# The first step of a fused two-layer kernel: the order of its loads, products, sums and copies

## The chip, the cores and the metric

The kernel runs on one core of a Trainium2 chip. A core has five engines with instruction streams of their own: PE (TensorE, matmuls and transposes), DVE (VectorE), ACT (ScalarE), POOL (GpSimd) and SP (SyncE, which here only issues DMAs). Each works through its stream in order and waits for semaphores of the others. The metric is device time in microseconds of one execution, lower is better. Before the change it was 2017.71 us (median of three, 2015.79 to 2018.18).

## The reference

The input has 2048 rows (4 sequences of 512) of 512 float32 values. Two layers are computed; each normalizes the rows and adds an attention and a mixture of experts that both read the normalized rows:

```python
xn = _layernorm(x)
x = x + _L0_attn_ref(xn, ...) + _L0_ffn_ref(xn, ...)
xn = _layernorm(x)
x = x + _L1_attn_ref(xn, ...) + _L1_ffn_ref(xn, ...)
```

The change touches the first normalization and the first attention. That attention has 16 heads of 128 and projects the normalized rows with Wq, Wlk and Wlv to queries, local keys and local values, each 2048 wide, with RMS norms and a rotation of queries and keys:

```python
q = (hidden_states @ Wq + bq).reshape(Bq, Sq, NH, D).transpose(0, 2, 1, 3)
q = apply_rope(rmsnorm(q, qn_w), pos)
lk = apply_rope(rmsnorm((hidden_states @ Wlk + blk).reshape(...)..., kn_w), pos)
lv = (hidden_states @ Wlv + blv).reshape(Bq, Sq, NH, D).transpose(0, 2, 1, 3)
```

## The kernel before

**Staging.** The rows lie in 16 tiles of 128 (`acc`), four tiles to a sequence. A tile is normalized to `xn` by `layernorm` (L226): statistics on DVE (L232 to L235), a power on POOL (L236), and the scaling on DVE (L247) or, where `scaled` is set, on ACT (L245, with one more POOL operation, L238). Its rows are then stored to DRAM (L250), transposed on PE (L255) and copied by ACT into `xnT` (L256). Rows 0 to 3 go the DVE way, rows 4 to 15 the ACT way.

The first attention runs in 32 steps: 8 groups of two heads, and in each group the four sequences. Step i projects one sequence on one group's 768 columns, makes scores and contexts, and meanwhile projects for step i+1. Jobs for other parts, such as the normalization of rows 8 to 15 in steps 0 and 1, are hung between (`jobs0`, L962 on).

**The projection.** `project` (L656) halves the 512 rows and the 512 inner elements and multiplies the four blocks with seven products in place of eight, by sums of blocks of x (`sums_x`, L667: `xs[0]` to `xs[3]`) and of the weights (`combine_weights`, L112: t3, b1 in place, t2, t4). A product (L681) covers 128 rows at a time (`c` is 0 or 1) and accumulates two matmuls, each of which the profile shows as two instructions. Products one and two (`first`, L710) read the plain blocks; six and seven (`second`, L720) read `xs1` with t2 and `xs2` with t3; four (`third`, L726) reads t4; five and three follow. After products one and two, `finish` (L688) squares the six heads' rows on ACT (L581), raises to −0.5 on POOL (L583, L584), rotates on DVE (L591 to L594) and scales on ACT (L695). `turn_queries` (L697) transposes the queries on PE.

**Order.** The program is written engine by engine in Python order, but a planner reorders the instructions of an engine by its estimate of when their inputs are there. `tc.keep_in_program_order(ins)` forbids that for one instruction: it stays behind the instruction written just before it on its engine. Before the change, of the opening, the norms of rows 0 to 3, their transposes, the four weight sums, the tables (`tables`, L201, POOL) and some POOL operations are pinned; products, sums of x, squares, copies and all later statistics are free.

The opening is written as: start rows 0 and 1, scale the norm weights (L197), products p1(0), p2(0), p1(1), then `rest` (L1082: rows 2 and 3, tables, and the loads of everything that follows), the adds of the first projection, p2(1), `finish(0)`, then

```python
entry_tables()
combine_weights(0)
bound()
unrotated()
sums_x()
first_logits(0)
second(0)
turn_queries(0)
second(1)
third()
```

**Queues.** Nearly all loads are issued by SP in written order: row 0, first half of wA, row 1, the norm weights qn_w and kn_w, second half of wA, bias A, rows 2 and 3, cos, sin, the two halves of wB, bias B, small ones, wr (the weights of the router's logits, `first_logits`, L941), then the stores of `xn` and the other loads.

**PSUM.** Banks are shared by tag: three "mm" (products), three "sc" (logits, scores), two "tr" (transposes).

Of the kernel before, what the change touches and what calls it, by code (L numbers as in the profile page):

```python
# [29 lines left out]
E = 8  # L30
# [19 lines left out]
def two_layers(ctx: ExitStack, tc: tile.TileContext, a: dict, out: bass.AP, large: bass.AP):  # L50
# [37 lines left out]
    def load_block(g, nm, between=None):  # L88
# [3 lines left out]
        for f in range(2):  # L92
            nc.sync.dma_start(out=w[:, ts(f, 2), :],
                              in_=a[nm][g, ts(f, 2 * P), :].rearrange("(k p) c -> p k c", p=P))
            if between:
                between(nm, f)
# [15 lines left out]
    def combine_weights(g):  # L112
# [4 lines left out]
        t2_, t3_, t4_ = (wpool.tile([P, 2, 3 * D], F32, tag=f"wT{x}", name=f"wT{x}_{g}", bufs=1) for x in (2, 3, 4))  # L117
        for o, x, y in ((t3_, b2_, b1), (b1, b1, w_a[:, 0:2, :]), (t2_, b2_, b1), (t4_, t2_, a2)):
            tc.keep_in_program_order(V.tensor_tensor(o, x, y, ALU.subtract))  # L119
        d = G.tensor_tensor(b2[:, 1, :], b2[:, 1, :], b2[:, 0, :], ALU.subtract)  # L120
        if g == 0:
            tc.keep_in_program_order(d)
        sums_w[g] = t2_, t3_, t4_
# [28 lines left out]
    def load_between(nm, f):  # L152
        if nm == "wA" and f == 0:
            load_x(1)
            for w, src in enumerate(("qn_w", "kn_w")):
                nc.sync.dma_start(out=nw[:, w, :], in_=a[src].partition_broadcast(P))

    def load_tables():
        for n in range(2, TC):
            load_x(n)  # L160
# [3 lines left out]
    load_x(0)  # L164
    w_ = [load_block(0, "wA", load_between)]
# [3 lines left out]
    w_.append(load_block(0, "wB", load_between))  # L169
# [5 lines left out]
    wr = load_few(sp0, "wr", 1 + E, a["wr9"])  # L175
# [50 lines left out]
    def layernorm(n, pool, bank, scaled=False, bufs=None):  # L226
# [5 lines left out]
        pin(V.bn_stats(st, acc[:, n, :]))  # L232
# [8 lines left out]
        def rows():  # L241
            tag = "ctx" if n in (2, 3) else "xn"
            xn = made["xn"] = (wk0 if n in (2, 3) else pool).tile([P, HID], F32, tag=tag, name=f"xn_{n}", bufs=bufs)
            if scaled:
                A.activation(xn, acc[:, n, :], AF.Identity, scale=mv[:, 1:2], bias=mv[:, 0:1])  # L245
# [6 lines left out]
        def turn():  # L252
# [3 lines left out]
            A.copy(xnT[:, :, ts(n, P)], tr.rearrange("p (k t) -> p k t", k=KC))  # L256
# [3 lines left out]
    def logits(b, w, m, pool, name, get, bank):  # L260
# [6 lines left out]
        A.copy(lr, lp)  # L267

        def turn():
            tr = bank("tr", f"trg_{name}_{b}")  # L270
            for t in range(TC):
                PE.transpose(tr[:, ts(t, P)], lr[:, ts(t, P)], ident)
# [303 lines left out]
    def squares(x, n, pool, name, extra=1.0):  # L576

        sq = pool.tile([P, D], F32, tag="sq", name=f"sq_{name}", bufs=1)
        ss = small.tile([P, n], F32, tag=f"ss{n}", name=f"ss_{name}", bufs=4)
        for h in range(n):  # L580
            A.activation(sq, x[:, h, :], AF.Square, accum_out=ss[:, h : h + 1])  # L581
        pin = tc.keep_in_program_order if name == "0_0" else (lambda x: x)
# [73 lines left out]
    def project(i):  # L656
# [10 lines left out]
        def sums_x():  # L667
# [1643 lines left out]
```

## Time and profile before

| | |
|---|---|
| median of three runs | 2017.71 us (2015.79 to 2018.18) |
| profiled execution | 2017.76 us |
| its span, first to last instruction | 2016.0 us |
| mean granted TensorE clock | 0.997 |
| DVE, ACT, POOL busy | 1513.7, 866.7, 743.2 us |
| DMA moved | 267.26 MB, 133 GB/s |
| PE busy in 0 to 36 us, 36 to 82 us, 82 to 145 us | 22.00, 42.91, 62.97 us |

The profile is that of one execution. "Busy" sums the time in which an engine worked on instructions. In a timeline row the numbers are start and duration in us, then engine, line, operation, the tile written and read, shapes and how many were merged; in brackets stands the idle time before it and who ended it. A window row gives the busy time of each engine in a stretch with the count of instructions.

### The profile page before, as it was taken

What the parts mean: (1) busy time and instruction counts of PE and PEld (TensorE: products, weight loads), DVE (VectorE), ACT (ScalarE), POOL (GpSimd) and SP (SyncE); (2) the same over time, 40 slices, a digit from 0 to 9 for tenths busy, and PEclk for the clock granted to TensorE, in tenths of its full rate; (3) what the DMA queues carried; (4) which work ended last, traced back from release to release, by engine and by line L of the source; (5) the groups of instructions that cost most, each with busy time, mean ns of one, the idle gap of its engine ahead of it and who ended that gap; (6) DMA issues with size and microseconds to landing.
All of it is one profiled execution on the core that took longest, in us unless ns stands there. A gap on an engine that the chain in (4) does not pass through costs nothing.

```text
span 2016.0 us, 28488 instructions
## 1 busy us (share of the span) xinstructions
PE 1976.1 (98%) x9358; PEld 1241.5 (62%) x9358; DVE 1513.7 (75%) x3696; ACT 866.7 (43%) x2600; POOL 743.2 (37%) x761
## 2 busy tenths in 40 slices
PE   7999999999999999999999999999999999999998
PEld 4666666777767767776667766666434445445443
DVE  7889977777776777787767788788696755565886
ACT  4554444444444444444444445545234432333332
POOL 4422244443332333333442344445204432333551
PEclk8999999999999999999999999999999999999999
DMA  7102133432433333344452222321307775775441
GB/s 257 70 32 63 33 131 111 155 116 95 139 111 122 120 123 136 106 134 158 152 182 99 96 65 82 90 80 70 128 22 247 258 257 194 266 254 173 155 155 69
DMA packets 98908, 267.26 MB, mean 133 GB/s; under 512 B 14400, under 2 KB 27840, under 8 KB 87488
## 3 DMA queue, kind: packets, MB, share of 16 engines
q0 software_dynamic: 27072, 148.91, 21.9%
q1 hardware_dynamic: 70528, 114.34, 16.9%
q10 hardware_dynamic: 1152, 2.10, 0.3%
q8 instruction: 77, 1.26, 0.3%
q14 instruction: 79, 0.65, 0.1%
HBM read 222.05 MB, written 42.73 MB: 131 GB/s over the span
## 4 chain that ended last, share of the span: by engine, by line
PE 84%; DVE 8%; ACT 2%; POOL 1%; issue 1%; DMA 1%; DVEq 0%; ACTq 0%; POOLq 0%
PE p L681 24%; PE hp_r L534 13%; PE st L773 4%; PE op L848 4%; PE st L1344 3%; PE po L1482 3%; PE cx L1358 3%; PE qp L1320 3%; PE sp L764 2%; PE ox L879 2%; PE o L1427 2%; PE ca L817 2%; PE trm_r L522 1%; PE oz L879 1%; PE trq L701 1%; PE cc L820 1%
## 5 line engine op out<-in xcount | busy, mean ns | idle before, releaser
L534 PE MATMUL hp_r<-we_r,xT_r 128*128 128x512 f32 (+1 forms) x592 | 224.7, 596 | 2.7 <-ACT xT_r L524 2.2
L486 POOL DMA_INDIRECT xr_r<-xnd,rows_r x72 | 87.7, 1218 | 345.1 <-PE trm_r L522 307.4
L781 POOL TENSOR_TENSOR lT<-lT,lmask 128x512 f32<-128x512 f32 (+1 forms) x128 | 152.4, 1199 | 122.5 <-ACT lT L777 122.1
L681 PE MATMUL p<-wT,x 128*128 128x384 f32 x512 | 179.7, 494 | 0.8 <-DVE wT L119 0.8
L681 PE MATMUL p<-wB,x 128*128 128x384 f32 x512 | 175.9, 488 | 0.8 <-DVE u L737 0.8
L681 PE MATMUL p<-wA,xnT 128*128 128x384 f32 x512 | 173.8, 490 | 0.7 <-DVE u L716 0.4
L581 ACT ACTIVATE sq<-qb 128x128 f32<-128x128 f32 x384 | 118.9, 310 | 91.7 <-DVE qb L730 45.6
L1346 ACT ACTIVATE pT<-st 128x1024 f32<-128x1024 f32 x128 | 123.3, 1015 | 59.3 <-PE st L1344 51.1
L534 PEld LDWEIGHTS hp_r<-we_r,xT_r 128*128 128x128 f32 (+1 forms) x592 | 83.1, 170 | 98.8 <-issue 92.4
L681 PEld LDWEIGHTS p<-wT,x 128*128 128x128 f32 x512 | 94.6, 193 | 63.3 <-issue 6.5
L681 PEld LDWEIGHTS p<-wB,x 128*128 128x128 f32 x512 | 93.7, 190 | 64.4 <-issue 9.6
L681 PEld LDWEIGHTS p<-wA,xnT 128*128 128x128 f32 x512 | 94.9, 192 | 62.1 <-DVE u L716 3.5
L695 ACT ACTIVATE qb<-qb,ss 128x128 f32<-128x128 f32 x256 | 81.9, 390 | 107.7 <-POOL ss L584 104.6
L524 ACT COPY xT_r<-trm_r 128x512 f32<-128x512 f32 x72 | 41.8, 580 | 194.3 <-PE hp_r L534 183.2
L773 PE MATMUL st<-qkT 128*128 128x256 f32 (+1 forms) x512 | 114.6, 354 | 1.5 <-ACT qkT L708 1.5
L777 ACT ACTIVATE lT<-st,ss 128x256 f32<-128x256 f32 (+1 forms) x128 | 48.9, 444 | 151.7 <-PE st L773 151.7
L551 POOL DMA_INDIRECT row_r<-yd,slot_r x64 | 72.8, 1137 | 73.9 <-DMA yd<-yr_r 21.5
L773 PEld LDWEIGHTS st<-qkT 128*128 128x128 f32 x512 | 92.2, 190 | 12.0 <-ACT qkT L708 1.7
L584 POOL TENSOR_TENSOR ss<-ss,nhalf 128x6 f32<-128x6 f32 x64 | 96.1, 1502 | 5.3
L848 PE MATMUL op<-Wo,cT 128*128 128x512 f32 x208 | 93.9, 596 | 1.3 <-DVE lv L745 1.2
L583 POOL TENSOR_SCALAR ss<-ss 128x6 f32<-128x6 f32 x64 | 31.3, 489 | 166.3 <-ACT sq L581 165.9
L681 PE MATMUL p<-wT,xnT 128*128 128x384 f32 x256 | 88.1, 486 | 0.0
(385 smaller groups left out, 4627.9 us busy)
## 6 DMA issues: line engine op xcount, KB each, us to landing
x<-xsd SPq DMA_DIRECT2D x112, 256.0 KB, 3.1
yd<-yr_r SPq DMA_DIRECT2D x72, 256.0 KB, 4.9
wA<-in_wA SPq DMA_DIRECT2D x16, 384.0 KB, 3.5
wB<-in_wB SPq DMA_DIRECT2D x16, 384.0 KB, 7.3
xnd<-xn SPq DMA_DIRECT2D x24, 256.0 KB, 2.2
accd<-acc SPq DMA_DIRECT2D x18, 256.0 KB, 2.1
acc<-in_x SPq DMA_DIRECT2D x16, 256.0 KB, 5.8
Wo<-in_Wo SPq DMA_DIRECT2D x8, 512.0 KB, 3.6
```

The costliest lines, as they stand in the source:

```text
L486: G.indirect_dma_start(out=out, out_offset=None, in_=src, in_offset=at_rows(idx))
L534: PE.matmul(hp[ts(h, m), :], lhsT=xT[:, k, ts(h, m)], rhs=w[:, ts(k, HID)], start=(k == 0), stop=(k == KC - 1))
L551: G.indirect_dma_start(out=x, out_offset=None, in_=self.yd, in_offset=at_rows(self.r.slot[:, k, n : n + 1]))
L581: A.activation(sq, x[:, h, :], AF.Square, accum_out=ss[:, h : h + 1])
L584: pin(G.tensor_tensor(ss, ss, nhalf[:, 0:n], ALU.pow))
L681: PE.matmul(p, lhsT=x[:, k, ts(c, P)], rhs=w[:, k, :], start=(k == 0), stop=(k == 1))
L695: A.activation(x[:, j, :], x[:, j, :], AF.Copy, scale=sq[t][:, j : j + 1])
L773: PE.matmul(st[:, ds((t % 2) * 256, n)], lhsT=qkT[:, HG + h, ts(t, P)], rhs=qkT[:, h, ds(t * P, n)], start=True, stop=True)
L781: G.tensor_tensor(dst, dst, lmask.rearrange("p a w j -> p (a w j)")[:, 0:n], ALU.mult)
L848: PE.matmul(op, lhsT=cT[:, h, ts(t, P)], rhs=wo[:, h, :], start=(h == 0), stop=(h == HG - 1))
L879: PE.matmul(p[:, ts(c, 256)], lhsT=left[:, ts(c, P)], rhs=right, start=new and c == 0, stop=True, skip_group_check=True)
L1346: A.activation(pt[:, ts(pair, 2), :], st, AF.Exp, scale=SCALE1)
```

## The change

All edits concern the opening, except one.

- Loads: rows 0 to 3 are issued first; then wA, bias A, qn_w and kn_w, cos and sin, wB; wr ahead of bias B.
- Rows 1 and 3 are normalized with `scaled` set. The statistics of rows 0 and 1 are written ahead of both scalings, and the opening, with `scale_weights`, `tables` and `rest`, is written ahead of the products (`begin`).
- `first` takes a generator `parts`: the transposes of rows 2 and 3, sums of x and weight sums are written between the products and adds of step 0.
- `sevenths` makes both halves of p7, in "sc" banks, behind the first logits and ahead of `turn_queries` and p6; `second` then adds them from there.
- Pinned now in step 0: products, sums of x, the adds of the first projection, the first squares, ACT's copies of rows 0 to 3, the copy and transposes of the first logits.
- The exception: the first statistic (L232) of rows 8 to 15 is pinned.

The diff, with unchanged lines cut (the line numbers are in its hunk headers):

```diff
--- before.py
+++ after.py
@@ -85,15 +85,13 @@
...
         return t
-    def load_block(g, nm, between=None):
+    def load_block(g, nm):
         w = wpool.tile([P, KC, 3 * D], F32, tag=nm, name=f"{nm}_{g}", bufs=1 if nm == "wA" else 2)
...
                               in_=a[nm][g, ts(f, 2 * P), :].rearrange("(k p) c -> p k c", p=P))
-            if between:
-                between(nm, f)
         return w
...
@@ -109,18 +107,21 @@
...
         return wo
-    def combine_weights(g):
+    def combine_weights(g, which=(0, 1, 2, 3)):
         (w_a, w_b), b2 = groups[g]
         a2, b1, b2_ = w_a[:, 2:4, :], w_b[:, 0:2, :], w_b[:, 2:4, :]
-        t2_, t3_, t4_ = (wpool.tile([P, 2, 3 * D], F32, tag=f"wT{x}", name=f"wT{x}_{g}", bufs=1) for x in (2, 3, 4))
-        for o, x, y in ((t3_, b2_, b1), (b1, b1, w_a[:, 0:2, :]), (t2_, b2_, b1), (t4_, t2_, a2)):
-            tc.keep_in_program_order(V.tensor_tensor(o, x, y, ALU.subtract))
-        d = G.tensor_tensor(b2[:, 1, :], b2[:, 1, :], b2[:, 0, :], ALU.subtract)
-        if g == 0:
-            tc.keep_in_program_order(d)
-        sums_w[g] = t2_, t3_, t4_
+        if g not in sums_w:
+            sums_w[g] = [wpool.tile([P, 2, 3 * D], F32, tag=f"wT{x}", name=f"wT{x}_{g}", bufs=1) for x in (2, 3, 4)]
+        t2_, t3_, t4_ = sums_w[g]
+        for n, (o, x, y) in enumerate(((t3_, b2_, b1), (b1, b1, w_a[:, 0:2, :]), (t2_, b2_, b1), (t4_, t2_, a2))):
+            if n in which:
+                tc.keep_in_program_order(V.tensor_tensor(o, x, y, ALU.subtract))
+        if 3 in which:
+            d = G.tensor_tensor(b2[:, 1, :], b2[:, 1, :], b2[:, 0, :], ALU.subtract)
+            if g == 0:
+                tc.keep_in_program_order(d)
     sums_w, out_w, out_t = {}, {}, {}
...
@@ -149,30 +150,25 @@
...
     wcol = small.tile([P, 2], F32, tag="wcol", name="wcol", bufs=1)
-    def load_between(nm, f):
-        if nm == "wA" and f == 0:
-            load_x(1)
-            for w, src in enumerate(("qn_w", "kn_w")):
-                nc.sync.dma_start(out=nw[:, w, :], in_=a[src].partition_broadcast(P))
-
     def load_tables():
-        for n in range(2, TC):
-            load_x(n)
+        for w, src in enumerate(("qn_w", "kn_w")):
+            nc.sync.dma_start(out=nw[:, w, :], in_=a[src].partition_broadcast(P))
         nc.sync.dma_start(out=cos, in_=a["c_cos"][:, :, 0:R])
         nc.sync.dma_start(out=sin, in_=a["c_sin"])
-    load_x(0)
-    w_ = [load_block(0, "wA", load_between)]
+    for n in range(TC):
+        load_x(n)
+    w_ = [load_block(0, "wA")]
     b_ = wpool.tile([P, 2, 3 * D], F32, tag="b2", name="b2_0")
...
     load_tables()
-    w_.append(load_block(0, "wB", load_between))
+    w_.append(load_block(0, "wB"))
+    wr = load_few(sp0, "wr", 1 + E, a["wr9"])
     nc.sync.dma_start(out=b_[:, 1, :], in_=a["bB"][0].partition_broadcast(P))
...
         nc.sync.dma_start(out=wcol[:, w : w + 1], in_=a[src].rearrange("(d o) -> d o", o=1))
-    wr = load_few(sp0, "wr", 1 + E, a["wr9"])
     bcmp = load(const0, "bcmp", [P, 1], a["bcmp"].partition_broadcast(P))
...
@@ -229,7 +225,9 @@
...
         st = small.tile([P, 6], F32, tag="st", name=f"st_{n}")
-        pin(V.bn_stats(st, acc[:, n, :]))
+        made_ = V.bn_stats(st, acc[:, n, :])
+        if n < TC or scaled and n >= 2 * TC:
+            tc.keep_in_program_order(made_)
         mv = small.tile([P, 2], F32, tag="mv", name=f"mv_{n}")
...
@@ -242,7 +240,7 @@
...
             if scaled:
-                A.activation(xn, acc[:, n, :], AF.Identity, scale=mv[:, 1:2], bias=mv[:, 0:1])
+                pin(A.activation(xn, acc[:, n, :], AF.Identity, scale=mv[:, 1:2], bias=mv[:, 0:1]))
             else:
...
@@ -253,7 +251,7 @@
...
                 pin(PE.transpose(tr[:, ts(k, P)], xn[:, ts(k, P)], ident))
-            A.copy(xnT[:, :, ts(n, P)], tr.rearrange("p (k t) -> p k t", k=KC))
+            pin(A.copy(xnT[:, :, ts(n, P)], tr.rearrange("p (k t) -> p k t", k=KC)))
         return rows, turn
@@ -264,12 +262,13 @@
...
         lr = pool.tile([P, S], F32, tag="lr", name=f"lr_{name}_{b}", bufs=1)
-        A.copy(lr, lp)
+        pin = tc.keep_in_program_order if name == "r0" and b == 0 else (lambda x: x)
+        pin(A.copy(lr, lp))
         def turn():
...
             for t in range(TC):
-                PE.transpose(tr[:, ts(t, P)], lr[:, ts(t, P)], ident)
+                pin(PE.transpose(tr[:, ts(t, P)], lr[:, ts(t, P)], ident))
             get(tr.rearrange("p (t k m) -> p t m k", k=KC, m=FEW)[:, :, 0:m, :])
...
@@ -577,9 +576,9 @@
...
         ss = small.tile([P, n], F32, tag=f"ss{n}", name=f"ss_{name}", bufs=4)
+        pin = tc.keep_in_program_order if name == "0_0" else (lambda x: x)
         for h in range(n):
-            A.activation(sq, x[:, h, :], AF.Square, accum_out=ss[:, h : h + 1])
-        pin = tc.keep_in_program_order if name == "0_0" else (lambda x: x)
+            pin(A.activation(sq, x[:, h, :], AF.Square, accum_out=ss[:, h : h + 1]))
         pin(G.tensor_scalar(ss, ss, D * 1e-6, extra, ALU.add, ALU.mult))
...
@@ -664,21 +663,26 @@
...
         u, qb, sq = {}, {}, {}
-        def sums_x():
-            if i < B:
-                V.tensor_tensor(xs[2], x11, x21, ALU.subtract)
-                V.tensor_tensor(xs[0], x21, x22, ALU.add)
-                V.tensor_tensor(xs[1], xs[0], x11, ALU.subtract)
+        fixed = tc.keep_in_program_order if i == 0 else (lambda x: x)
+
+        def sums_x(which=(2, 0, 1, 3)):
+            if i < B and 2 in which:
+                fixed(V.tensor_tensor(xs[2], x11, x21, ALU.subtract))
+            if i < B and 0 in which:
+                fixed(V.tensor_tensor(xs[0], x21, x22, ALU.add))
+            if i < B and 1 in which:
+                fixed(V.tensor_tensor(xs[1], xs[0], x11, ALU.subtract))
+            if i < B and 3 in which:
                 d = G.tensor_tensor(xs[3], x12, xs[1], ALU.subtract)
...
                     nc.sync.dma_start(out=xsd[b, n], in_=xs[n].rearrange("p k t -> p (k t)"))
-        def product(nm, x, w, c):
-            p = psum("mm", f"{nm}_{i}_{c}")[:, 0 : 3 * D]
+        def product(nm, x, w, c, bank="mm"):
+            p = psum(bank, f"{nm}_{i}_{c}")[:, 0 : 3 * D]
             for k in range(2):
-                PE.matmul(p, lhsT=x[:, k, ts(c, P)], rhs=w[:, k, :], start=(k == 0), stop=(k == 1))
+                fixed(PE.matmul(p, lhsT=x[:, k, ts(c, P)], rhs=w[:, k, :], start=(k == 0), stop=(k == 1)))
             return p
...
@@ -707,21 +711,35 @@
...
             A.activation(qkT[:, HG + h, :], tr, AF.Copy, scale=turned[:, 0:1])
-        def first(between=lambda: None):
+        def first(parts=None):
             u2, qb[0] = tmp("u2"), wk0.tile(rows3, F32, tag="qb", name=f"qb0_{i}")
             p1, p2 = (lambda c: product("p1", x11, w_a[:, 0:2, :], c)), (lambda c: product("p2", x12, w_a[:, 2:4, :], c))
-            made = [p1(0), p2(0), p1(1)]
-            between()
+            made = [p1(0), p2(0), p1(1)] if i else [p1(0)]
             for c in range(2):
-                V.tensor_tensor(u2[:, c, :], made.pop(0), b2[:, 0, :], ALU.add)
-                V.tensor_tensor(qb[0][:, c, :], made.pop(0) if made else p2(1), u2[:, c, :], ALU.add)
+                if parts:
+                    next(parts)
+                fixed(V.tensor_tensor(u2[:, c, :], made.pop(0), b2[:, 0, :], ALU.add))
+                if parts:
+                    made = [p2(c)]
+                    next(parts)
+                    if c == 0:
+                        made.append(p1(1))
+                fixed(V.tensor_tensor(qb[0][:, c, :], made.pop(0) if made else p2(1), u2[:, c, :], ALU.add))
+            if parts:
+                next(parts)
             finish(0)
+
+        early = {}
+
+        def sevenths():
+            for c in range(2):
+                early[c] = product("p7", xs2, sums_w[g][1], c, "sc")
         def second(c):
...
             V.tensor_tensor(u2[:, c, :], product("p6", xs1, t2_, c), u2[:, c, :], ALU.add)
-            V.tensor_tensor(u3[:, c, :], product("p7", xs2, t3_, c), u2[:, c, :], ALU.add)
+            V.tensor_tensor(u3[:, c, :], early[c] if early else product("p7", xs2, t3_, c), u2[:, c, :], ALU.add)
         def third():
...
@@ -750,7 +768,7 @@
...
         xs0, xs1, xs2, xs3 = (xs[n] for n in range(4))
-        return qkT, sums_x, first, second, third, fourth, fifth, turn_queries, turn_keys
+        return qkT, sums_x, first, second, third, fourth, fifth, turn_queries, turn_keys, sevenths
     def scores(i, h, qkT):
@@ -941,9 +959,8 @@
...
             V.tensor_reduce(lg0[:, ts(b, TC), :], rows_[:, :, 1:, :], AX.X, ALU.add)
-        lr, turn = logits(b, wr, 1 + E, sp0, "r0", get, psum)
-        turn()
-        row_w[b] = lr
+        row_w[b], turn = logits(b, wr, 1 + E, sp0, "r0", get, psum)
+        return turn
     def second_logits(b, pool, bank):
...
@@ -965,7 +982,7 @@
...
         if b > 1:
-            jobs0.append(((i, 4), lambda b=b: first_logits(b)))
+            jobs0.append(((i, 4), lambda b=b: first_logits(b)()))
         for t in (0, 1, 3.5, 4):
...
@@ -1075,15 +1092,37 @@
...
     load_sums(0)
-    qkT, sums_x, first, second, third, fourth, fifth, turn_queries, turn_keys = project(0)
-    start_sequence(0)
-    start_sequence(1)
-    scale_weights()
+    qkT, sums_x, first, second, third, fourth, fifth, turn_queries, turn_keys, sevenths = project(0)
+    start = [layernorm(n, sp0, psum, n % 2 == 1) for n in range(2)]
+
+    def begin():
+        start[0][0]()
+        start[1][0]()
+        start[0][1]()
+        start.append(layernorm(2, sp0, psum))
+        start[1][1]()
+        start.append(layernorm(3, sp0, psum, True))
+        start[2][0]()
+        start[3][0]()
+        scale_weights()
+        tables()
+        rest()
+
+    def parts():
+        start[2][1]()
+        yield
+        start[3][1]()
+        yield
+        sums_x((2, 0))
+        yield
+        combine_weights(0, (0,))
+        yield
+        sums_x((1,))
+        combine_weights(0, (1,))
+        yield
+
     def rest():
         nonlocal wk, wv, bkv, cmask, lmask, eidx, row, part
-        start_sequence(2)
-        start_sequence(3)
-        tables()
         for n in range(TC, TC + 2):
...
@@ -1102,16 +1141,20 @@
...
         part = load(const, "part", [P, 1], a["c_part"])
-    first(rest)
+    begin()
+    first(parts())
+    combine_weights(0, (2,))
+    turn_ = first_logits(0)
+    sevenths()
     entry_tables()
-    combine_weights(0)
+    sums_x((3,))
+    turn_queries(0)
+    second(0)
+    turn_()
+    combine_weights(0, (3,))
+    second(1)
     bound()
     unrotated()
-    sums_x()
-    first_logits(0)
-    second(0)
-    turn_queries(0)
-    second(1)
     third()
...
@@ -1125,7 +1168,7 @@
...
     next(comp[0])
-    first_logits(1)
+    first_logits(1)()
     for i, (g, b) in enumerate(steps):
...
@@ -1141,7 +1184,7 @@
...
             load_sums(i + 1)
-            qkT, sums_x, first, second, third, fourth, fifth, turn_queries, turn_keys = project(i + 1)
+            qkT, sums_x, first, second, third, fourth, fifth, turn_queries, turn_keys, _ = project(i + 1)
             first()
...
             if b == 2 and g + 1 in groups:
```

## The prediction

> **What bounds the kernel now.** I read the busy shares first.
>
> ```profile
> PE 1976.1 (98%) x9358; PEld 1241.5 (62%) x9358; DVE 1513.7 (75%) x3696; ACT 866.7 (43%) x2600; POOL 743.2 (37%) x761
> ```
>
> TensorE is idle for 2016.0 − 1976.1 = 39.9 us. A change of order wins only idle time, and time in which PE runs below full clock. I then asked for stretches. PE is idle 14.0 us in the first 36, 3.1 us from 36 to 82, 0.03 us from 82 to 145, and 6.5 us after 1950. The change touches the opening and the steps just behind it, so its field is 0 to 145 us:
>
> ```profile
> 20.00:22.00 2.00, 0.66 (x4) 0.42 (x4) 2.00 (x5) 1.62 (x7) 0.00 (x0) 1.00 0.77 165
> 22.00:24.00 2.00, 0.00 (x0) 0.00 (x0) 2.00 (x6) 0.14 (x2) 1.69 (x2) 0.75 0.85 270
> 26.00:28.00 2.00, 1.18 (x5) 0.77 (x4) 1.91 (x3) 0.58 (x1) 2.00 (x2) 0.50 1.06 401
> 28.00:30.00 2.00, 2.00 (x4) 1.03 (x4) 2.00 (x7) 0.10 (x1) 0.59 (x1) 0.50 1.05 384
> 32.00:34.00 2.00, 2.00 (x6) 1.07 (x5) 0.95 (x7) 0.00 (x0) 0.20 (x1) 0.69 0.56 175
> 34.00:36.00 2.00, 2.00 (x8) 1.21 (x7) 1.91 (x6) 0.99 (x2) 1.58 (x4) 1.00 0.08 31
> ```
>
> The columns are PE, PEld, DVE, ACT, POOL busy, then PE's granted clock, DMA share, GB/s. After the hole at 22 to 24 the clock is 0.50, from about 23.0 (0.75 over 22 to 24) to 33.2 (0.69 over 32 to 34). The PE timeline gives the cause and the price:
>
> ```profile
> 16.01 1.47 PE L681 MATMUL p<-wA,xnT 128*128 128x384 f32 x4
> 18.84 1.06 PE L265 MATMUL lg_r<-xnT,wr 128*32 128x512 f32 x8 [1.36 <-ACT xnT L256]
> 20.61 0.66 PE L272 MATMUL trg_r<-ident,lr_r 128*128 128x128 f32 x4 [0.70 <-ACT lr_r L267]
> 24.73 0.47 PE L701 MATMUL trq<-ident,qb 128*128 128x128 f32 x1 [3.46 <-ACT qb L695]
> ...
> 27.52 8.24 PE L681 MATMUL p<-wT,x 128*128 128x384 f32 x16 [0.82 <-DVE wT L119]
> 35.60 0.81 PE L681 MATMUL p<-wT,xnT 128*128 128x384 f32 x2
> ```
>
> The sixteen instructions from 27.52 are products six and seven. They wait for the third weight sum (L119, from 26.18). Four instructions, one product, take 1.29 us at full clock (35.60 to 38.18 for the eight of p4), so sixteen should take 5.2, not 8.1.
>
> The last view is DVE against PE behind that:
>
> ```profile
> 36.00:82.00 46.00, 42.91 (x227) 30.05 (x226) 44.80 (x135) 28.88 (x94) 18.80 (x29) 1.00 0.33 113
> 82.00:145.00 63.00, 62.97 (x315) 41.78 (x314) 50.43 (x140) 33.82 (x112) 20.16 (x26) 1.00 0.14 52
> ```
>
> From 36 to 82 DVE is idle for 1.2 us of 46. Whatever PE gains earlier must pass through this full engine. From 82 PE binds, DVE has 12.6 us of room in 63, and a lead kept to 82 should last to the end.
>
> **The change, part by part.** My marker is the start of p4 (35.60 before).
>
> *Rows ahead of weights.* Rows 0 to 3 are 1.05 MB. The first statistic starts at 3.43 when row 0 has landed, and by 14.1 the second half of wB (issued 7.6, 6.5 to landing) is there: 3.28 MB in all, so 3.0 MB in 10.7 us, 282 GB/s. Rows 1, 2, 3 then land near 4.4, 5.3, 6.2, where the trace has 6.32 and 10.48 for rows 1 and 2. wA comes 0.79 MB later: its halves near 8 and 9.5, not 4.5 and 8.5. qn_w and kn_w go behind bA on SP's queue, to about 11 (6.4 and 7.2 before). DVE meets them in nws (L199), ahead of the first u2; that add needs p1(0) at 11.4 anyway, so this costs nothing, and 1 us if they land at 12.5. wr moves ahead of bB and lands by about 15; the logits need it at 17. bB's user, the bias difference on POOL, came at 25.66.
>
> *Norms of rows 1 and 3 on ACT.* Each leaves DVE (0.55 us, L247; once 0.94), and adds 0.26 on POOL (L238) and 0.81 on ACT (L245). Row 0's chain is as before: statistic 3.43, power on POOL to 5.25, xn at 5.83. Row 1 follows at about 7.6 (before 8.70), row 3 at 10.1 (before 15.4). PE's order is now T0, T1, p1(0), T2, p2(0), T3, p1(1), p2(1). T1 ends at 8.7. The weight loads of before stand 0.64 apart until 12.8, so p1(0) takes 4 x 0.64 = 2.6, to 11.4. T2 takes 1.1 cold; p2(0) ends at 13.8, T3 at 14.3, p1(1) at 15.6, p2(1) at 16.9 (17.48 before). Gain so far 0.6.
>
> *Sums in fixed order.* DVE runs qb(0), xs2, xs0, u2, t3, qb(1), xs1, b1, rotation, t2. With the durations of the rows (0.55, 0.88, 0.68, 0.55, 0.95, 0.55, 0.68, 0.94, 1.7, 0.95) from copy T3 at 14.9, this puts t3 at 17.9, qb(1) at 18.4, t2 near 22.6. Before, t2 ended at 27.46. The 5 us come from bn4, the weights' reduce and the wait in front of them, and from a start of the sums at 14.9 in place of 18.82.
>
> *Sevenths first.* Logits run 16.9 to 18.0 and p7 (xs2, t3) 18.0 to 20.6: 2.6 us of PE work moved into what was a hole. They sit in two "sc" banks, the logits in the third; nobody else wants one before wB at 41.63.
>
> *Pinned squares, copy and queries.* p6(0) now stands behind the queries' transposes. Squares of qb(1) end at 19.8; POOL 0.21 + 1.72, ACT's four scales 1.28: transposes end at 23.3. The copy of the logits is pinned behind the scales too, 23.6, where it was 20.55; nothing needs it before trg. So p6(0) runs 23.3 to 24.6, trg 0.44, p6(1) to 26.3. t4 stands behind the reduce of trg (25.3) and ends at 26.2. **p4 starts at 26.4, 9.2 us earlier.**
>
> *The clock.* Row: 2.04 us of PE work from 16.2 to 19.6 kept full clock; about 1.0 from 19.6 to 23.0 lost it; 2.3 of 3.4 from 26.4 did not restore it. The new order has some 1.6 of work in 19.6 to 23.0 (p7's last 1.0, then the queries' transposes), with one hole of about 1.6 from 20.6: a little nearer the first. I take full clock. With half, p6 costs 2.6 more and the lead is 6.6. The Trainium skill, "TensorE: Matmul & The Clock Gate", Part 1, says that a wholly idle window of about 3.4 us halves the clock; by that rule no hole here is long enough and the sum is 2010.3, while the rows, which tie it to the amount of work, leave 2012.9 open.
>
> *Later statistics in place.* Of rows 8 to 15, the statistics of 8 to 11 ran by 61.3 us and those of 12 to 15 from 72 to 82 (L232, 0.67 each, with 0.17 and 0.14 behind it), though the transposes of the last four came at 108 to 127. These 3 to 4 us leave the full stretch for one with room.
>
> *What eats the lead.* DVE does 68.1 us of work up to 82. I take off 1.1 (two norms) and 3.4 (statistics), and add 0.8 for sums beside POOL. That leaves 64.4. By my order DVE idles some 7.6 us until 22.6, one more until 27, and 1.2 to 3 afterwards: 74.2 to 76 in place of 82, a lead of 6.0 to 7.8. By PE it is 9.2. I take **7.5**: near DVE's upper end, since some of its work can wait beyond 82. Moved statistics might cost from nothing to 20 us (rival three).
>
> Beside POOL: xs2 took 0.88 at 18.82 during a table product, 0.67 at 52.67; t2 took 1.28 with xs3 on POOL, other sums 0.95. The skill's "GPSIMD Engine Reference", 8. Key points, says the two share SBUF interfaces and contend when VectorE has two SBUF inputs. It speaks against this change, which puts xs2, xs0 and t3 beside the tables; by the rule every such sum is slower, by these rows 0.2 to 0.3 each.
>
> **Sum.** The profiled execution took 2017.76, span 2016.0, and 1.76 around it; the median is 2017.71, the same. 2017.76 − 7.5 = **2010.3**.
>
> **Rivals.**
> One, *half given back*: DVE stays the bound, or the clock halves again. Lead 6.0 less 1 to 3 for stalls of rows 4 to 7: xn6 needs xn4's buffer, and a store took 6.3 us under load (41.26). Gives 2013 to 2016, say 2014. Chance 0.20. For it: DVE's 44.80 of 46.
> Two, *no gain*: the opening is faster, but p6 behind the queries and the full DVE return all of it. 2016 to 2020, say 2017.5. Against it: 2.9 us of half clock and 3.5 us of hole are real in the rows. Chance 0.12.
> Three, *slower*: a pinned statistic starts a chain of 0.67 + 0.17 + 0.14 on DVE, 0.55 + 0.26 on POOL, 0.81 on ACT, 2.6 us, before the transposes of rows 8 to 15, and PE stands in order behind them. It decides from 7.5 / 8 = 0.94 us of PE wait per row. At 1.6 each: 12.8 − 7.5 = +5.3, 2023. Against it: DVE's room from 82 on, and transposes that stand tens of us behind their statistics. Chance 0.12.
> Four, *more*: PE's 9.2 holds and part of the 3.1 idle goes too: 2005 to 2008. Chance 0.06.
>
> **How the numbers follow.** The forecast (2008 to 2013) has 0.50. The range 2006.5 to 2018.5 leaves out rival three, a third of two and half of four: 0.19. About 0.2%, 4.0 us, can be told from no change. Faster: 0.50 + 0.06 + half of rival one = 0.66. Same: half of one, two, a little of three = 0.25. Slower 0.09.
>
> **What would show it.** Right: p7 near 18, p4 near 26.4, clock 1.00 from 20 to 36, no statistic of rows 12 to 15 before the second step, PE idle in 0 to 36 near 8 us. Wrong: p6 waiting long for the queries (POOL's power late), clock 0.5 between 23 and 30, PE idle over 5 us in the stretch up to the second step, or waits of transposes L255 for xn in the first two steps.

## The result, and the profile after

The changed kernel took **2025.8 us** (median of 6, 2023.54 to 2028.16) where the kernel before took 2016.13 (median of 6, on the same chip). The ratio is 1.0047, with a 95% interval of 1.0034 to 1.006: **slower by about 9.7 us**, where 7.5 us of gain were forecast. The profiled execution took 2028.16 with a span of 2026.3, the longest of the six.

The busy shares of the changed kernel's page:

```profile
PE 1982.1 (98%) x9358; PEld 1244.1 (61%) x9358; DVE 1510.7 (75%) x3694; ACT 868.2 (43%) x2602; POOL 745.7 (37%) x763
```

PE is busy 6.0 us longer with the same 9358 instructions, at a granted clock of 0.995 in place of 0.997, so part of the loss is clock; its idle time is 44.2 us in place of 39.9.

The stretches of the opening, with the columns of before (PE, PEld, DVE, ACT, POOL, granted clock, DMA share, GB/s):

```profile
22.00:24.00 2.00, 1.15 (x6) 0.74 (x7) 1.92 (x6) 1.86 (x6) 2.00 (x4) 1.00 0.93 296
24.00:26.00 2.00, 2.00 (x7) 1.17 (x6) 0.99 (x4) 0.42 (x1) 2.00 (x3) 0.61 1.05 401
26.00:28.00 2.00, 2.00 (x6) 1.27 (x5) 2.00 (x5) 1.50 (x2) 1.08 (x4) 0.54 1.00 371
28.00:30.00 2.00, 2.00 (x12) 1.57 (x11) 1.94 (x6) 0.12 (x1) 0.00 (x0) 1.00 0.97 285
```

This half clock lasts some 3.4 us, not 10 as before. But two more such stretches follow, of 3.4 us each, where the kernel before has none: one behind a wait for the queries of the next step, one behind the wait at wB shown below.

```profile
38.29 0.48 PE L705 MATMUL trq<-ident,qb 128*128 128x128 f32 x1 [2.37 <-ACT qb L699]
```

```profile
38.00:40.00 2.00, 1.71 (x8) 1.71 (x9) 1.92 (x3) 1.46 (x5) 0.00 (x0) 0.52 1.02 327
40.00:42.00 2.00, 2.00 (x6) 1.09 (x5) 0.69 (x1) 0.66 (x2) 0.00 (x0) 0.62 1.04 332
70.00:75.00 5.00, 5.00 (x25) 4.04 (x24) 3.62 (x8) 1.82 (x4) 0.10 (x1) 0.78 0.14 52
```

The PE timeline of the changed kernel in the first stretch:

```profile
17.88 2.85 PE L685 MATMUL p<-wT,x 128*128 128x384 f32 x8 [0.97 <-DVE wT L120]
22.60 0.33 PE L705 MATMUL trq<-ident,qb 128*128 128x128 f32 x1 [1.87 <-ACT qb L699]
...
23.64 1.98 PE L685 MATMUL p<-wT,x 128*128 128x384 f32 x4
25.41 1.06 PE L271 MATMUL trg_r<-ident,lr_r 128*128 128x128 f32 x4
26.26 2.25 PE L685 MATMUL p<-wT,x 128*128 128x384 f32 x4
28.34 0.63 PE L601 MATMUL wt<-ident,lr_r 128*128 128x128 f32 x4
28.81 0.49 PE L253 MATMUL trx<-ident,xn 128*128 128x128 f32 x3
29.14 2.75 PE L685 MATMUL p<-wT,xnT 128*128 128x384 f32 x8
```

The sevenths start at 17.88 and p4 at 29.14: the opening did become 6.5 us faster at the marker. The loss comes behind it:

```profile
36.00:82.00 46.00, 40.57 (x186) 28.22 (x186) 38.19 (x107) 20.76 (x72) 14.76 (x17) 0.93 0.27 92
82.00:145.00 63.00, 57.62 (x296) 38.51 (x294) 48.77 (x148) 34.22 (x114) 21.12 (x31) 1.00 0.12 43
```

DVE, which was full from 36 to 82, now has 7.8 us of room there. PE does not use it: it idles 5.4 us in this stretch and 5.4 in the next, where it had idled 3.1 and 0.03.

For what follows I use a second marker, the first score matmul of each step, and give its **lag** behind the kernel before in one profiled execution of each kernel (minus is earlier). Lags are counted from the profiler's zero, some 10.5 us ahead of the first instruction; from the first instruction, as the timelines are, they differ by up to 0.3 us. The changed kernel is 4.8 us ahead at step 0, 3.1 late at step 1, 7.2 late at step 2; it keeps this to step 29 (6.5), and is 9.7 late at step 30 and 10.1 at step 31. So there are two losses, **12.0 us in steps 0 and 1**, and **some 3.5 us in steps 29 and 30**.

What PE waits for in step 0 is in its timeline (the words in brackets: idle time before, and who ended it):

```profile
60.10 4.68 PE L685 MATMUL p<-wT,x 128*128 128x384 f32 x14
67.64 1.10 PE L616 MATMUL wB<-wd,ones_sq 128*128 128x512 f32 x2 [2.85 <-DVE wd L613]
...
71.00 1.11 PE L253 MATMUL trx<-ident,xn 128*128 128x128 f32 x4
...
93.66 0.66 PE L253 MATMUL trx<-ident,xn 128*128 128x128 f32 x4 [2.01 <-ACT xn L243]
```

and in the DVE timeline of the same kernel:

```profile
66.58 0.92 DVE L613 TENSOR_SCALAR wd<-ident,w 128x128 f32<-128x128 f32 x4
67.36 0.67 DVE L228 BATCH_NORM_STATS2 st<-acc 128x6 f32<-128x512 f32 x1
```

The pinned statistic of row 8 starts straight behind the last wd, the instruction that stands ahead of it in the text. Before, the same stretch of PE read:

```profile
62.69 0.66 PE L255 MATMUL trx<-ident,xn 128*128 128x128 f32 x4
64.83 1.78 PE L773 MATMUL st<-qkT 128*128 128x256 f32 x8 [1.49 <-ACT qkT L708]
66.45 0.81 PE L681 MATMUL p<-wT,x 128*128 128x384 f32 x2
67.10 0.49 PE L799 MATMUL trs<-ident,s 128*128 128x128 f32 x3
67.71 1.10 PE L617 MATMUL wB<-wd,ones_sq 128*128 128x512 f32 x2
```

There row 8's transposes (62.69) and other work stood between the transposes wt and the matmul wB, and covered the chain on DVE and ACT that makes wd. With the pin they can't: row 8 is normalized only behind wd, its transposes come at 71.00, and PE runs dry in front of wB.

### The profile page after: what moved, and what is told of

Same layout as the page of the kernel before. It is cut to its first block, busy times and chain, and to the rows that moved or that the text cites. A ratio compares the mean times of both kernels' runs of the same rounds, so it can differ in the third digit from the quotient of the medians.

```text
span 2026.3 us, 28496 instructions
## 1 busy us (share of the span) xinstructions
PE 1982.1 (98%) x9358; PEld 1244.1 (61%) x9358; DVE 1510.7 (75%) x3694; ACT 868.2 (43%) x2602; POOL 745.7 (37%) x763
## 4 chain that ended last, share of the span: by engine, by line
PE 82%; DVE 8%; ACT 2%; POOL 1%; issue 1%; DMA 0%; ACTq 0%; DVEq 0%; POOLq 0%
PE p L685 23%; PE hp_r L533 12%; PE st L791 4%; PE op L866 3%; PE st L1387 3%; PE po L1525 3%; PE cx L1401 3%; PE qp L1363 3%; PE sp L782 2%; PE ox L897 2%; PE o L1470 2%; PE ca L835 2%; PE oz L897 1%; PE trm_r L521 1%; PE trq L705 1%; PE trk L711 1%
## 5 line engine op out<-in xcount | busy, mean ns | idle before, releaser
L791 PEld LDWEIGHTS st<-qkT 128*128 128x128 f32 x512 | 92.2, 191 | 10.2 <-issue 0.5
```

The lines of the kernel that those rows point to most:

```text
L791: PE.matmul(st[:, ds((t % 2) * 256, n)], lhsT=qkT[:, HG + h, ts(t, P)], rhs=qkT[:, h, ds(t * P, n)], start=True, stop=True)
```

## The experiments

Each ran in five rounds against the kernel before on the same chip. A first table has all; the lags are relative to before. A lag is of one execution, and the executions of one kernel differ by up to 5.4 us in time: the profiled one of e3 is the fastest of its eleven.

| kernel | median us | ratio (95%) | lag at step 0, 1, 2 | at step 31 |
|---|---|---|---|---|
| changed | 2025.8 | 1.0047 (1.0034 to 1.006) | −4.8, +3.1, +7.2 | +10.1 |
| e1 changed, copies free | 2024.41 | 1.0034 (1.0022 to 1.0046) | −5.3, +3.2, +7.4 | +6.8 |
| e2 changed, statistics free | 2016.58 | 0.9998 (0.9989 to 1.0007) | −6.4, −4.7, −3.7 | −2.2 |
| e3 both free | 2014.58 | 0.9989 (0.998 to 0.9998) | −7.3, −5.6, −4.6 | −5.5 |
| e4 before, statistics pinned | 2030.67 | 1.0066 (1.0054 to 1.0079) | +1.3, +8.6, +12.7 | +11.9 |
| e5 pinned two places earlier | 2021.63 | 1.0029 (1.0018 to 1.004) | −1.2, +4.5, +6.3 | +5.4 |
| e6 before, rows 8 to 11 pinned | 2023.35 | 1.0035 (1.0023 to 1.0047) | +0.5, +6.2, +6.2 | +5.5 |
| e7 both free, sixths first | 2015.42 | 0.9996 (0.9987 to 1.0005) | −1.7, −2.1, −2.1 | −2.7 |
| e8 before, copies pinned | 2018.51 | 1.0011 (1.0002 to 1.002) | −0.1, −0.1, −0.1 | +2.3 |
| e9 pinned, ahead of wd | 2021.05 | 1.0018 (1.0009 to 1.0027) | −6.9, −1.3, +2.2 | +2.2 |
| e10 free, ahead of wd | 2013.56 | 0.9982 (0.9973 to 0.9991) | −6.7, −5.0, −4.0 | −4.4 |
| e11 before, sevenths ahead | 2021.57 | 1.0019 (1.001 to 1.0028) | +3.0, +3.5, +4.5 | +4.0 |
| e12 before, rows first | 2015.19 | 0.9991 (0.9982 to 1.0) | −3.2, −3.2, −3.2 | −3.0 |
| e13 pinned, written early | 2022.8 | 1.0029 (1.0018 to 1.004) | +0.7, +5.5, +5.5 | +4.8 |
| e14 free, written early | 2020.66 | 1.0019 (1.001 to 1.0028) | −1.3, +2.6, +2.6 | +1.7 |

Theory A: the pinned statistics of rows 8 to 15 cost steps 0 and 1. Rival B: the rest of the change costs there (p6 behind the queries, fixed sums). Theory C, beside A: the pins of the copies cost in step 29. The condition `n < TC` in `layernorm` is true for rows 0 to 3 of the *second* layer as well, which run there.

The diffs below are cut to the lines that matter.

**e1 to e4: which pin.** e1 pins the copies of the first layer alone; e2 takes the exception out; e3 does both; e4 puts the exception, and nothing else, into the kernel before.

```diff
 e1, e3:  copied = A.copy(xnT[:, :, ts(n, P)], ...)
-         pin(copied)
+         if pool is sp0:
+             pin(copied)
 e2, e3:
-         if n < TC or scaled and n >= 2 * TC:
-             tc.keep_in_program_order(made_)
+         pin(made_)
 e4 (kernel before):
-         pin(V.bn_stats(st, acc[:, n, :]))
+         made_ = V.bn_stats(st, acc[:, n, :])
+         if n < TC or scaled and n >= 2 * TC:
+             tc.keep_in_program_order(made_)
```

> The changed kernel, with ACT's copies of transposed rows pinned in the first layer alone, and free again for rows 0 to 3 of the second layer. Theory C (the pinned copy in step 30 stands behind four scales, PE waits 3.18 us for its bank and then runs twelve products at half clock): the lag of 3.2 us that appears between steps 30 and 31 goes, 2025.8 - 3.3 = about 2022.5, and the lag of 7 us from steps 0 and 1 stays. Rival (that lag is chance, or the scale would delay PE anyhow): no change, 2024 to 2027.

> The changed kernel, with the first statistic of rows 8 to 15 free again. Theory A (the statistics in place start chains that PE's transposes wait for): the first scores keep their lead of some 5 us over the kernel before through steps 0 and 1, so 12 us come back: about 2014. Theory B (the planner orders steps 0 and 1 differently because the opening ends earlier, whatever the statistics do): under 3 us come back, 2023 to 2026.

> Both of these at once: statistics of rows 8 to 15 free, copies pinned in the first layer alone. Theories A and C add up: 2025.8 - 12 - 3.3 = about 2010.5, faster than the kernel before by 5 to 6 us. Under theory B: about 2021.

> The kernel before, with one edit of the change alone: the first statistic of rows 8 to 15 pinned. Theory A: 8 to 12 us are lost in steps 0 and 1, 2024 to 2028. Theory B: within 2 us of 2016.

e3 lies at 2014.58 and e2 at 2016.58, 4.1 and 2.6 above A's values, and further from B's. e4 is 13.5 us slower than the 2017.18 of before, more than A's 2024 to 2028 allowed: the exception alone, without any of the rest, costs more than the whole change. **A is shown, B falls.** Step 0 of before, then of e4, each from its first score matmul to that of step 1:

```profile
58.30:99.10 40.80, 39.18 (x208) 27.19 (x206) 36.55 (x117) 23.47 (x73) 18.41 (x28) 1.00 0.20 73
```

```profile
59.40:107.50 48.10, 41.28 (x207) 28.05 (x205) 37.01 (x112) 22.70 (x72) 17.26 (x21) 0.96 0.14 51
```

Of the 7.3 us more, 5.2 are idle PE (6.82 against 1.62) and 2.1 the same matmuls at a clock of 0.96. The wait at wB is 2.28 here, too; the waits of transposes for xn that can be seen are 0.83 and 0.93, and the queries' transposes wait 1.77 for the last row's copy.

For C the two timelines of PE in step 29 (counted from 0; the expectations of e1 and e8 call it step 30 and the step before the last) say what happens, before and after:

```profile
1345.14 0.63 PE L255 MATMUL trx<-ident,xn 128*128 128x128 f32 x4 [1.80 <-DVE xn L247]
1345.60 4.04 PE L681 MATMUL p<-wB,x 128*128 128x384 f32 x12
```

```profile
1353.10 1.12 PE L253 MATMUL trx<-ident,xn 128*128 128x128 f32 x4 [3.18 <-ACT xnT L254]
1354.01 6.54 PE L685 MATMUL p<-wB,x 128*128 128x384 f32 x12
```

Before, ACT made the copy at 1340.76, between two squares. Pinned, it stands behind the four scales of the queries (1351.30, 1.28 us), which wait 2.57 us for POOL. PE waits 3.18 us for the bank, where it had waited 1.80 for xn, and then runs the twelve products at a lower clock. In e1 the lag stays 6.8 through steps 29 to 31. The median of e1 alone would not show it (2024.41 against 2025.8, intervals overlapping, and within the rival's range); e8 below does.

**e5 to e8: is it the place, and what is the opening worth.** e5 writes the statistics two places ahead of the rest of each row (base e1). e6 pins rows 8 to 11 only, in the kernel before. e7 is e3 with p7 behind p6 again. e8 is the kernel before with C's pin alone.

```diff
 e5:          jobs0.append(((i, t), lambda n=b * TC + t: start_sequence(n)))
+             if 2 * TC <= b * TC + t + 2 < NT:
+                 jobs0.append(((i, t), lambda n=b * TC + t + 2: make_statistic(n)))
 ...
+    make_statistic(2 * TC)
+    make_statistic(2 * TC + 1)
     first_logits(1)()
 e6:
+        if n < TC or scaled and 2 * TC <= n < 3 * TC:
+            tc.keep_in_program_order(made_)
 e7:
-    sevenths()
 e8:
+            if pool is not sp0:
+                pin(copied)
```

> The changed kernel with the second layer's copies free, and with the first statistic of rows 8 to 15 still pinned, but written two places earlier (rows 8 and 9 ahead of the second sequence's logits, row 10 with row 8's place, and so on), while the scaling, the transposes and the copy of each row stay at their places. Theory A1 (the pin costs by its late place: statistic, sums, power, scale and transposes are a chain of 2.6 us and more that starts only at its place, with TensorE's queue behind the transposes): the chain is over by then, nearly all of the loss goes, as in the kernel with both free: about 2015 us (2013 to 2018). Theory A2 (any pin among these rows costs, because it takes the planner's freedom on VectorE away, wherever it stands): the loss stays, about 2024 us (2021 to 2026).

> The kernel before with the first statistic of rows 8 to 11 alone pinned in its place (those of the first step), rows 12 to 15 free. With rows 8 to 15 pinned the time rose by some 14 us. If each row costs by its own chain: about half, some 2023 us (2021 to 2026). If the first step alone has the loss (the second sequence's weights wB and the row sums come late there and push everything): nearly all, 2027 to 2031 us. If it's the second step: 2016 to 2019 us.

> The kernel with statistics and copies free, but the seventh products at their old place behind the sixth. If the sevenths ahead of the sixths bring the opening's gain: TensorE has no work between the logits (17.9) and the queries' transposes (22.6), a hole of near 5 us, the clock is halved for the sixths, and the fourth products come 3 to 5 us later; with the lead kept, about 2018 us (2016.5 to 2020). If they only fill a hole that is paid for later on VectorE anyway: 2014 to 2016 us, as with them ahead.

> The kernel before with the copies of rows 0 to 3 of the second layer pinned on ScalarE (those that the condition n < TC catches besides the first layer's), nothing else. Theory C (the pinned copy falls behind four scales in the step before the last, TensorE waits 3.2 us and its clock is halved): 3.3 us more, about 2019.5 us (2018 to 2021). Rival: no cost by itself, 2015 to 2017.5 us.

e6 met the case "about half": step 0 is 5.7 us longer, step 1 is as before, to 0.1 us. Each step pays for its own rows. e5 lies in A2's range, at its lower end, and far from A1's. Yet it doesn't bear out A2's reason: steps 0 and 1 lose 7.5 us in place of e1's 12.7, so the earlier place pays there, while the opening lost 4.1 of e1's lead. Two more statistics stand in that opening now, and its clock is half for 6.8 us (37.6 to 44.4) in place of 3.4, about 1.7 of the 4.1; the rest was not separated. e8 confirms C by itself: nothing until step 29, then +2.3 us, 1.0011, with the same wait of 3.18 us. In e7 PE waits 5.27 us for the queries and p6 runs at half clock (5.08 us for its eight instructions, against 2 x 1.46 in e3):

```profile
22.57 1.49 PE L706 MATMUL trq<-ident,qb 128*128 128x128 f32 x4 [5.27 <-ACT qb L700]
23.86 5.08 PE L686 MATMUL p<-wT,x 128*128 128x384 f32 x8
```

p4 comes at 31.79, 3.5 us later than in e3, and the scores of step 0 5.6 later. At step 31 only 2.8 of that are left, and the medians don't tell the two apart. Half of what the sevenths win is given back in steps 0 and 1.

**e9 to e12: a smaller move, and parts alone.** e9 (pinned, base e1) and e10 (free, base e3) write each statistic as the first job of its old place, ahead of the part of the compression that stands there. e11 writes the sevenths ahead of the logits in the kernel before, e12 loads rows 1 to 3 ahead of the weights there.

```diff
 e9, e10:
+    for n in range(2 * TC, NT):
+        jobs0.append(((n // TC - 2, n % TC), lambda n=n: make_statistic(n)))
     for b in range(1, B):
 e11:  sums_x()
+      sevenths()
       first_logits(0)
 e12:
-    load_x(0)
+    for n in range(TC):
+        load_x(n)
```

> The changed kernel with the second layer's copies free; the first statistic of rows 8 to 15 is still pinned and written at its old places, but as the first thing there, ahead of the part of the compression (the four wd, or the products and sums of entT) that stands there too. The trace of the pinned kernels has row 8's statistic straight behind the last wd (67.4 after 67.2), and TensorE then waits 2.3 to 2.9 us at wB with no transposes left to put before it. Theory P (a pinned statistic takes over the wait of the instruction written before it; the place decides): rows 8 and 12 come before wd again, their transposes go ahead of wB, its wait shrinks to about 1 us, and 2 to 4 us come back: 2020 to 2022.5 us. Rival (the pin by itself, or the rows 9 to 11 and 13 to 15 alone): 2024 us as in the kernel with only the copies free (2022.5 to 2026).

> The same writing order with the statistics free (and the second layer's copies free). A free statistic is placed by the planner's estimate, not by the line it is written at: within 1 us of the kernel with both free, 2013.5 to 2015.5 us. If the written place matters for free ones too, it would be over 2 us away from that.

> The kernel before with one part of the change alone: the seventh products of step 0 are written ahead of the first logits, into banks of their own; nothing else moves, and nothing new is pinned. In the kernel with all the opening's parts, putting them back behind the sixth cost 3.5 us at the fourth products and 5.6 us at the first scores, but only 1.5 us of the span. If this part carries the gain by itself: 2 to 4 us, 2012 to 2014 us. If it needs the others (t3, which they read, is made only at 22.97 to 23.9 here, 0.8 us ahead of the queries' transposes): 2015 to 2017 us, no change.

> The kernel before with only the loads of rows 1 to 3 put ahead of the weights of the first group; nothing else moves. Rows 1 and 2 land 2 and 4 us earlier (statistics now at 6.3 and 10.5), wA later. If the rows' arrival bounds the opening: transposes of row 3 some 1 to 2 us earlier and 1 to 2 us off the time, 2014 to 2016 us. If the later wA takes it back (first products at about 11 us either way): 2016 to 2018 us.

e9 is 4.6 us better than e1 at step 31 (3.6 of it in steps 0 and 1) and within P's range, so the place has a price. But P's reason held only in half. Row 8's statistic ran at 50.7 and its transposes at 55.8, ahead of wB, yet wd came no earlier than 64.5, and PE still waited there (put down to an aggregate, L232, right behind wd):

```profile
55.77 0.66 PE L253 MATMUL trx<-ident,xn 128*128 128x128 f32 x4 [0.19 <-ACT qkT L714]
65.83 2.04 PE L618 MATMUL wB<-wd,ones_sq 128*128 128x512 f32 x2 [2.79 <-DVE mv L232]
```

e11 went the other way than both of its cases, to **slower**: the sevenths stood in PE's queue before their sum t3 was there, and the logits stood behind them:

```profile
24.54 4.65 PE L681 MATMUL p<-wT,x 128*128 128x384 f32 x8 [6.88 <-DVE wT L119]
29.12 1.07 PE L265 MATMUL lg_r<-xnT,wr 128*32 128x512 f32 x8
```

(logits at 18.84 before). In the changed order, with t3 made earlier and behind the logits, they fill a hole (e3 against e7). e12, a plain order of loads, has the logits at 17.07 and p4 at 32.76, 2.8 us earlier, and keeps all of it to the end (−3.0; 2.45 in the medians, and the ratio's interval ends at 1.0). About 1 of the 2.8 comes from a half clock of 6.8 us there in place of 10.2.

**e13 and e14: all eight early.** What was open: whether the rest of the loss is place too. Both write row 8 to 10's statistics in the opening, row 11's ahead of the second logits, rows 12 to 15's in step 0, with eight buffers for the small results; pinned in e13 (base e1), free in e14 (base e3).

```diff
-        st = small.tile([P, 6], F32, tag="st", name=f"st_{n}")
+        st = small.tile([P, 6], F32, tag="st", name=f"st_{n}", bufs=8)
 ...
     start_sequence(5)
+    make_statistic(8)
     fourth()
+    make_statistic(9)
 ...
```

> The changed kernel with the second layer's copies free; the first statistic of all eight rows is pinned, but written about where the planner puts it when it is free: rows 8 to 10 in the opening (after row 5's start, the fourth and the fifth part of the projection), row 11 ahead of the second sequence's logits, rows 12 to 15 as the first job at the four places of the first step. The small results get eight buffers in place of three. If the place is all of it: as with free statistics, 2012.5 to 2016.5 us. If a pin among these rows costs by itself: 2019 to 2024 us.

> The same text and buffers with the eight statistics free (and the second layer's copies free), as a control: 2012.5 to 2015.5 us, as the other kernels with free statistics. If the larger rings or the places matter for free statistics, it is over 2 us away from those.

e13 lies in the range named for a pin that costs by itself. But the control e14, without that pin, missed its own range by 5 us, so e13's time doesn't show this. With free statistics, e14 made all eight by 61.3 us and lost in the opening: PE waits 3.12 us for the queries at 38.55, and is 17.10 us busy between 36 and 60 where e10 has 21.76:

```profile
36.00:60.00 24.00, 17.10 (x85) 11.39 (x86) 20.53 (x64) 12.00 (x35) 11.84 (x22) 0.93 0.49 171
```

Why it did is not shown: e14 makes rows 12 to 15 earlier than e3 (next table), but rows 8 to 10 later, and also rows 6 and 7 (31.7 and 36.6 against 24.4 and 25.2). The starts of the eight statistics beside what each stretch lost:

| kernel | rows 8 to 11 | rows 12 to 15 | lag at step 0 | lost in step 0 | in step 1 |
|---|---|---|---|---|---|
| before | 37.7 to 60.6 | 72.1 to 81.7 | 0 | 0 | 0 |
| e3, free | 30.9 to 50.6 | 63.2 to 75.9 | −7.3 | 1.7 | 1.0 |
| e14, free | 40.4 to 44.9 | 49.9 to 60.6 | −1.3 | 3.9 | 0.0 |
| e13 | 40.8 to 54.2 | 67.8 to 93.2 | +0.7 | 4.8 | 0.0 |
| e5 | 31.5 to 77.1 | 83.5 to 128.4 | −1.2 | 5.7 | 1.9 |
| e9 | 50.7 to 84.5 | 92.3 to 133.3 | −6.9 | 5.6 | 3.5 |
| e6 | 69.1 to 92.9 | 94.0 to 99.8 | +0.5 | 5.7 | 0.0 |
| e4 | 69.6 to 93.4 | 124.3 to 143.9 | +1.3 | 7.3 | 4.1 |

Step 1 loses nothing with rows 12 to 15 made in step 0, pinned (e13) or free (e6), 1.9 with two of them made in step 1 (e5), and 3.5 to 4.1 with three or four. In that step the loss goes with the place, and a pin at an early place cost nothing. (The 1.0 of e3 goes with its lead, see the next section.) Step 0 is not as clean: e14 loses 3.9 there with no pin and no late statistic. Part of it is moved work: PE is busy 42.76 us in its step 0 with 219 instructions, where before it is 39.18 with 208, and idle for 1.94 against 1.62. In e13 PE idles 4.04 us in step 0, 3.66 of it in one wait (70.25) for the scores' copy on ACT, which stands behind scales of the queries that wait for POOL. How much of the 5.6 to 7.3 in step 0 is place, and whether the pin adds something of its own, stays open (e13 lies 2.1 us above e14 in the medians, with intervals that meet). In e14, which of its two edits, the buffers or the places, moved the statistics wasn't tried.

## Why the prediction was wrong

**The step that failed is "Later statistics in place".** It took 3.4 us off DVE's budget as a gain. DVE did lose the work (38.19 of 46 in place of 44.80), but the stretch lost 12.0 us, 4.1 of it in the next step, by a place in PE's order that no DVE budget sees. The reason given was the distance of "tens of us" between statistics and transposes. It was there because the statistics ran early; the pin cuts it to 3.6 us (67.36 to 71.00).

**Rival three** had the right mechanism and nearly the right gross price, 12.8 against 11.4 in e4 (1.3 to 12.7) and 12.0 in the changed kernel, at a chance of 0.12. The place within it was wrong: waits of the transposes for xn are 3.7 us by the waits from 30 to 155, and 3.9 are at wB, which has lost the work in front of it. Over steps 0 and 1 of the changed kernel PE idles 7.0 us more than before and is busy 5.0 us more, about 1.7 of that by the half clock at 68.8 to 72.2; the rest of the 5.0 was not traced. So "from 0.94 us of PE wait per row" was no test: a row need not wait itself to cost.

**The pinned copies of rows** got no price. For those of the first layer no run shows one by itself. The condition's second use, 1300 us later, was not looked for: some 3.5 us in the changed kernel's trace, where the clock is half for 6.8 us behind the wait, and 2.3 in e8, where it is half for 3.4.

**The opening.** Sums in fixed order held: t3 ended at 17.8 (17.9), t2 at 23.0 (near 22.6), p7 started at 17.88 (18.0). p4 came at 29.14, not 26.4: p6 took 1.98 and 2.25 in place of 1.3 each, at half clock, trg 1.06 in place of 0.44, and wt and the first transposes of row 4 stand ahead of p4 (0.8), which the order by hand had left out. The clock was left open at 2.6 us, with full clock as the choice. That choice took the window 19.6 to 23.0 over from the kernel before; in the changed kernel's trace the half clock follows the window 21.0 to 24.4, with 1.6 us of PE work. (The cold window from 26.4 in the kernel before held 2.6 us of work, not 2.3.) *Rows ahead of weights* was valued at 0.6 us with the norms; p2(1) ended at 15.9, 1.6 earlier than before, and e12 shows a lead of 3.0 for the loads alone, of the parts tried the one that keeps all it wins.

**What eats the lead.** The marker's 9.2 was to become 7.5. Without the two bad pins (e3) the lead is 7.3 at step 0, falls to 4.6 by step 2, and ends at 5.5. In kind this is rival one, a lead partly given back. Of the 1.7 lost in step 0, PE's longer work is 1.1 and its idle time 0.6. e10 and e2 take the same 42.5 and 46.2 us for steps 0 and 1 as e3, against 40.8 and 45.2 before, while e7, with less lead, takes 40.3 and 45.2: so the better opening runs into a limit there, which no run isolates. In e3 PE's waits are 0.94 for the scores' copy and 0.94 and 1.01 for wd, chains that end on DVE and ACT. By the medians less is left than in that profiled execution: 2014.58, 1.1 in a thousand under before (the ratio of the table); the best kernel of the study, e10 at 2013.56, is 1.8 in a thousand under it.

## What to carry to other kernels

An instruction pinned to its written place can take over the wait of whatever is written ahead of it on its engine, as row 8's statistic did behind the last wd. Before pinning one that is "not needed yet", look at what hangs behind it on the busy engine, and which hole that work fills now; its distance to its user in the old trace is no reserve, since the old place made it. And look up every caller of a condition that turns a pin on: here `n < TC` was true again a whole layer later.

## What the runs showed of the hardware

**The clock's edge depends on the moment.** e9 and e10 run this stretch in the same order and wait the same 1.86 us for the queries, 0.27 us apart. First e9, then e10:

```profile
22.48 0.33 PE L707 MATMUL trq<-ident,qb 128*128 128x128 f32 x1 [1.86 <-ACT qb L701]
...
23.52 1.89 PE L687 MATMUL p<-wT,x 128*128 128x384 f32 x4
```

```profile
22.75 0.33 PE L706 MATMUL trq<-ident,qb 128*128 128x128 f32 x1 [1.86 <-ACT qb L700]
...
23.79 1.46 PE L686 MATMUL p<-wT,x 128*128 128x384 f32 x4
```

In e9 the granted clock is then 0.60 and 0.54 (24 to 26, 26 to 28), in e10 1.00. In each of the sixteen traces all changes of the granted clock lie whole multiples of 3.41 us apart (changed kernel: 24.44, 27.85, 38.09, 41.50, 68.81, 72.22), and this grid lies differently from trace to trace. The window ahead of e9's half clock, 21.00 to 24.41, holds 1.67 us of PE work; on e10's grid, counted on from its first change at 11.98, the same hole falls into 18.81 to 22.22 with 2.08 us and 22.22 to 25.63 with 2.62.

Over all such windows of the sixteen traces, from the first full clock to a few us before the end: at full clock up to 1.40 us of PE work always brought the half clock, 1.44 to 1.91 us sometimes, and more never. At half clock, windows with up to 2.59 us stayed there, and those from 2.90 us on were followed by full clock.

The Trainium skill, "TensorE: Matmul & The Clock Gate", Part 1, calls the window in which activity is watched free-running. That fits the pair. Its state table, by which an idle window of about 3.4 us brings the half clock, does not show in this pair: the longest idle time ahead of e9's half clock is 1.86 us.

**Sums beside POOL.** xs2, xs0 and t3 took 1.16, 0.94 and 1.43 us beside the tables, where the rows of before, used in the prediction, were 0.88, 0.68 and 0.95.
